# Two per-position convolutions in which the operands of the small products change places: x positions held in the array, the weights moved past them, eight products next to each other

## The chip, the core and the metric

The kernel runs on one core of a Trainium2 chip. The core has a matrix engine (TensorE, PE), a vector engine (DVE), a scalar engine (ACT), GpSimd (POOL), a queue engine that issues DMAs (SyncE, SP), an on-chip memory of 128 partitions (SBUF), a small accumulator memory of eight banks that TensorE writes (PSUM), and DRAM. The metric is the time of one execution on the device, in microseconds. A matrix product takes a stationary operand (loaded first) and a moving operand (streamed past it). A product written in fp32 is run as two loads and two matmul records.

## The reference

Two layers, each `x + conv(gn(x))`. The convolution has its own weights for each batch and position, made by a small network:

```python
S2, B, CI, CO, L, K, A, H = (32, 32, 64, 64, 256, 3, 16, 128)
h = relu(_ln(z @ W1 + b1, g1, be1))
w = (h @ W2 + b2).reshape(B, L, CI, CO, K)
hb = relu(_ln(z @ Wb1 + bb1, gb1, beb1))
bias = (hb @ Wb2 + bb2).transpose(0, 2, 1)
xp = pad(x, ((0, 0), (0, 0), (0, 0), (1, 1)))
x_uf = stack([xp[..., i:i + L] for i in range(K)], axis=-1)
out = einsum('sbilk,bliok->sbol', x_uf, w) + bias[None]
```

`x` has the shape (32 samples s, 32 batches b, 64 channels, 256 positions l), fp32, 67 MB. `gn` takes 32 groups of 8 positions; mean and variance of a group are over all batches, channels and the 8 positions, for each sample.

## The kernel before, in words

Partitions hold (two batches, channel). The work goes over 16 pairs of batches, within a pair over 4 chunks of 64 positions, and within a chunk over 3 taps.

For each tap, `make_weights` makes the weights w[i, o, l] of 64 positions: for each of the 64 outputs o and each batch of the pair, one product with the slice of W2 for that output as the stationary operand (128 hidden x 64 channels in) and the 64 hidden vectors as the moving one (L215). Eight outputs fill a PSUM bank; DVE takes each bank out, adds b2 and writes it to `w` with the output innermost (L222). Three banks (`ps_g`) rotate.

Then `convolve` runs the tap's small products (L236): for each position and each batch, w at that position (64 x 64) is the stationary operand and x at the shifted position (64 channels x 32 samples) the moving one. The taps add up in four banks (`ps_c`). The two batches use the upper and the lower half of the partitions. The next tap's weights are made ahead of a tap's products.

After the third tap, `finish` adds the four banks to x plus bias in place on DVE (L283). In the first layer it also takes the result into running means and squared deviations (`stats`, L118 to L128: DVE, ACT and POOL in turn). `join_stats` makes the group mean and inverse deviation from them with a matrix of 1/128. Before the first layer the same `stats` runs over the whole of x.

POOL normalizes a chunk of x (`normalized`, L204 and L205) and adds the bias (L315). `prepare` makes the hidden vectors and the bias for the next pair, one step after each tap. SP loads a pair's x in one DMA of 4 MB, and stores the result in one. The order on each engine is the planner's, with the order of the program as priority.

Of the kernel before, what the change touches and what calls it, by code (L numbers as in the profile page):

```python
# [12 lines left out]
statistics while they are on chip.  # L13
"""
# [9 lines left out]
FP = mybir.dt.float32  # L24
# [4 lines left out]
DRAM = bass.MemoryType.DRAM  # L29

# [3 lines left out]
LC = 64  # L34
# [5 lines left out]
def conv_layers(ctx: ExitStack, tc: tile.TileContext, x: bass.AP, layers: list, out: bass.AP):  # L40
# [3 lines left out]
    NP = B // 2  # L44
    NCH = L // LC
    GC = LC // E
    NB = LC // 16
    OG = 512 // LC
    assert 2 * C == P and 16 * S == 512 and NB == 4
# [3 lines left out]
    xp = ctx.enter_context(tc.tile_pool(name="x", bufs=2))  # L53
    xnp = ctx.enter_context(tc.tile_pool(name="xn", bufs=2))
# [5 lines left out]
    ps_c = ctx.enter_context(tc.tile_pool(name="ps_c", bufs=NB, space=PSUM))  # L60
    ps_p = ctx.enter_context(tc.tile_pool(name="ps_p", bufs=1, space=PSUM))

    # Centers a column over the 128 partitions; averages it.
    center = const.tile([P, P], FP, name="center")
    make_identity(nc, center)
    nc.vector.tensor_scalar(center, center, 1.0 / P, None, ALU.subtract)
    average = const.tile([P, P], FP, name="average")
    nc.vector.memset(average, 1.0 / P)
    eps = const.tile([P, 1], FP, name="eps")
    nc.vector.memset(eps, EPS)  # L70

    run_mean = const.tile([P, S, G], FP, name="run_mean")
    run_m2 = const.tile([P, S, G], FP, name="run_m2")
    gmean = const.tile([P, S, G], FP, name="gmean")
    rstd = const.tile([P, S, G], FP, name="rstd")

    def rows(t, j):
        return t[:, 2 * j : 2 * j + 2].rearrange("s b c l -> (b c) s l")

    x1 = [dram.tile([P, S, L], FP, name=f"x1_{j}") for j in range(NP)]  # L80

# [24 lines left out]
    def stats(j, y, g0, ng):  # L106
        """Takes y [P, S, ng * E], of pair j, into the running statistics of groups g0 and on."""
        d = prep1.tile([P, S // 2, GC * E], FP, tag="sd", name="sd")
        for h in range(2):
            ss = slice(h * S // 2, (h + 1) * S // 2)  # L110
            ye = y[:, ss].rearrange("p s (g e) -> p s g e", e=E)
            de = d[:, :, : ng * E].rearrange("p s (g e) -> p s g e", e=E)
            mean = run_mean[:, ss, g0 : g0 + ng]
            m2 = run_m2[:, ss, g0 : g0 + ng]
            shape = [P, S // 2, ng]
            m = mean if j == 0 else prep2.tile(shape, FP, tag="sm", name="sm")
            q = m2 if j == 0 else prep2.tile(shape, FP, tag="sq", name="sq")
            nc.vector.tensor_reduce(m, ye, AX.X, ALU.add)  # L118
            nc.scalar.mul(m, m, 1.0 / E)  # L119
            nc.gpsimd.tensor_tensor(de, ye, m[:, :, :, None].to_broadcast(shape + [E]), ALU.subtract)  # L120
            nc.scalar.activation(de, de, AF.Square)  # L121
            nc.vector.tensor_reduce(q, de, AX.X, ALU.add)  # L122
            if j:
                nc.vector.tensor_tensor(m, m, mean, ALU.subtract)  # L124
                nc.vector.scalar_tensor_tensor(mean, m, 1.0 / (j + 1), mean, ALU.mult, ALU.add)  # L125
                nc.vector.tensor_tensor(m2, m2, q, ALU.add)  # L126
                nc.scalar.activation(m, m, AF.Square, scale=(E * j / (j + 1)) ** 0.5)  # L127
                nc.vector.tensor_tensor(m2, m2, m, ALU.add)  # L128

    def join_stats():  # L130
        """gmean and rstd, the same on every partition."""
        n = E * NP
        flat = {k: v.rearrange("p s g -> p (s g)") for k, v in (("m", run_mean), ("q", run_m2), ("g", gmean), ("r", rstd))}
        for h in range(S * G // 512):
            c = slice(h * 512, (h + 1) * 512)
            pm = ps_p.tile([P, 512], FP, tag="pp", name="pm")
            nc.tensor.matmul(pm, average, flat["m"][:, c], start=True, stop=True)  # L137
            nc.scalar.copy(flat["g"][:, c], pm)
            d = prep1.tile([P, 512], FP, tag="hsq", name="sdev")
            nc.vector.tensor_tensor(d, flat["m"][:, c], flat["g"][:, c], ALU.subtract)  # L140
            nc.scalar.activation(d, d, AF.Square)
            v = prep1.tile([P, 512], FP, tag="hc", name="svar")
            nc.vector.scalar_tensor_tensor(v, flat["q"][:, c], 1.0 / n, d, ALU.mult, ALU.add)
            pv = ps_p.tile([P, 512], FP, tag="pp", name="pv")
            nc.tensor.matmul(pv, average, v, start=True, stop=True)
            nc.scalar.activation(flat["r"][:, c], pv, AF.Sqrt, bias=eps)
            nc.vector.reciprocal(flat["r"][:, c], flat["r"][:, c])  # L147

    def prepare(par, t, j, res):
        """The hidden vectors and the bias of pair j into res, in steps for the tensor engine."""  # L150
        N = 2 * L
        A = par["z"].shape[0]
        zt = prep2.tile([A, N], FP, tag="zt", name="zt")
        nc.sync.dma_start(out=zt, in_=par["z"][:, j * N : (j + 1) * N])
        for net in ("w", "b"):
            w, b, g, be = t[net]
            p1 = ps_p.tile([P, N], FP, tag="pp", name="p1")
            nc.tensor.matmul(p1, w, zt, start=True, stop=True)
            h = prep1.tile([P, N], FP, tag="hh", name="hh")
            nc.scalar.activation(h, p1, AF.Identity, bias=b)  # L160
            yield
            p2 = ps_p.tile([P, N], FP, tag="pp", name="p2")
            nc.tensor.matmul(p2, center, h, start=True, stop=True)  # L163
            hc = prep1.tile([P, N], FP, tag="hc", name="hc")
# [191 lines left out]
```

## Time and profile before

| | |
|---|---|
| median of 3 runs | 8146.04 us (8134.46 to 8150.21) |
| span of the profiled execution | 8109.2 us |
| TensorE busy, matmul records | 6764.3 us, 197136 |
| DVE busy | 4705.8 us |
| POOL busy | 2349.0 us |
| ACT busy | 661.3 us |
| moved by DMA | 375.27 MB, mean 46 GB/s |
| mean granted TensorE clock | 0.852 |

The span runs from the first to the last instruction of one profiled execution; no other time of that execution is given, and the median of the runs is 37 us above its span. In the rows, "PE" is a matmul and "PEld" the load of its stationary operand; L215 is line 215; "pc<-xn,w" is what is written and what is read; "128x512 f32" are partitions and elements; the mean of one instruction is in ns. "PEclk" is the granted TensorE clock in tenths of full speed, in 40 equal slices of the span.

### The profile page before, as it was taken

The page shows a single profiled execution, that of the slowest core. Times are in us where ns is not written, and L with a number is a line of the kernel's source. Part 1 is how long each engine was busy: PE and PEld are TensorE (multiplying, and loading weights), DVE is VectorE, ACT ScalarE, POOL GpSimd, SP SyncE. Part 2 cuts the span into 40 slices and gives each one's busy share as a digit, 9 for nine tenths or more (in the row PEclk, how much of TensorE's full clock was granted, in tenths as well). Part 3 has the DMA queues.
Part 4 walks back from the last instruction along what each step waited for, and adds up shares of the span by engine and source line. Part 5 has one row for each costly group of instructions (what it writes and reads, how often), then busy time and mean ns, then how long its engine had stood idle before and what let it go on. Part 6 is the DMA issues. An engine that isn't in the chain of part 4 may idle for free.

```text
span 8109.2 us, 402907 instructions
## 1 busy us (share of the span) xinstructions
PE 6764.3 (83%) x197136; PEld 6501.6 (80%) x197136; DVE 4705.8 (58%) x5199; ACT 661.3 (8%) x1118; POOL 2349.0 (29%) x1094
## 2 busy tenths in 40 slices
PE   2006888888888888888888889999999999999998
PEld 1005888788887888888878789999999999999998
DVE  7996555555555555555555545555555555555554
ACT  3331000000000000000000000000000000000000
POOL 3443322222322222222222313222222222322222
PEclk8556888788888888788878879999999999999999
DMA  4331110111001110111011110111111111111111
GB/s 151 110 104 43 45 45 3 44 45 44 16 32 45 45 41 6 44 45 44 3 44 45 45 75 4 45 45 45 46 46 46 46 46 46 49 47 40 45 45 45
DMA packets 208263, 375.27 MB, mean 46 GB/s; under 512 B 4352, under 2 KB 201280, under 8 KB 201792
## 3 DMA queue, kind: packets, MB, share of 16 engines
q1 hardware_dynamic: 206656, 349.49, 12.9%
q8 instruction: 1540, 25.23, 1.3%
q14 instruction: 67, 0.55, 0.0%
HBM read 215.26 MB, written 134.22 MB: 43 GB/s over the span
## 4 chain that ended last, share of the span: by engine, by line
PE 75%; DVE 11%; POOL 11%; issue 2%; ACT 1%; DMA 0%; SPq 0%; DVEq 0%; POOLq 0%; ACTq 0%
PE pc L236 40%; PE pg L215 33%; POOL xn L205 4%; POOL xn L204 3%; DVE run_m L128 2%; DVE sq L122 2%; POOL sd L120 2%; DVE sm L118 2%; POOL xt L315 2%; DVE sm L124 1%; DVE w L222 1%; DVE run_mean L125 1%; PE p L170 1%; DVE run_m L126 1%; PE p L163 1%
## 5 line engine op out<-in xcount | busy, mean ns | idle before, releaser
L222 DVE TENSOR_TENSOR w<-pg,b 128x512 f32<-128x512 f32 x3072 | 2987.6, 1075 | 2304.3 <-PE pg L215 2295.4
L215 PE MATMUL pg<-hTw,w 128*64 128x64 f32 x98304 | 3226.9, 231 | 658.0 <-DVE w L222 630.4
L215 PEld LDWEIGHTS pg<-hTw,w 128*64 128x64 f32 x98304 | 3142.4, 146 | 721.4 <-DVE w L222 663.3
L236 PEld LDWEIGHTS pc<-xn,w 64*64 64x64 f32 x98304 | 3291.3, 149 | 231.1 <-issue 185.7
L236 PE MATMUL pc<-xn,w 64*64 64x32 f32 x98304 | 3347.4, 231 | 68.2 <-issue 65.3
L204 POOL TENSOR_TENSOR xn<-xt,gmean 128x2048 f32<-128x2048 f32 (+1 forms) x320 | 534.4, 1712 | 2718.3 <-PE pc L236 2682.2
L205 POOL TENSOR_TENSOR xn<-xn,rstd 128x2048 f32<-128x2048 f32 (+1 forms) x320 | 730.0, 2311 | 2.9 <-DVE rstd L147 2.9
L120 POOL TENSOR_TENSOR sd<-xt,sm 128x1024 f32<-128x1024 f32 x240 | 486.5, 2027 | 506.5 <-DVE sq L122 391.3
L283 DVE TENSOR_TENSOR xt<-pc,xt 128x512 f32<-128x512 f32 x512 | 329.9, 686 | 478.2 <-PE pc L236 478.2
L315 POOL TENSOR_TENSOR xt<-xt,bias 128x2048 f32<-128x2048 f32 x128 | 578.6, 4530 | 0.0
L137 PE MATMUL pm<-run_mean,average 128*128 128x512 f32 x8 | 6.4, 890 | 463.2 <-DVE run_mean L125 462.3
L199 POOL MEMSET xn<- 128x32 f32 x32 | 4.0, 125 | 1304.2 <-PE pc L236 1304.2
L124 DVE TENSOR_TENSOR sm<-sm,run_mean 128x128 f32<-128x128 f32 x240 | 129.3, 539 | 434.6 <-POOL sd L120 434.6
L137 PEld LDWEIGHTS pm<-run_mean,average 128*128 128x128 f32 x8 | 1.6, 249 | 465.1 <-issue 462.5
L121 ACT ACTIVATE sd<-sd 128x1024 f32<-128x1024 f32 x256 | 270.5, 1057 | 867.9 <-POOL sd L120 867.9
L195 POOL MEMSET xn<- 128x32 f32 x32 | 4.0, 125 | 1091.6 <-PE pc L236 1091.6
L122 DVE TENSOR_REDUCE sq<-sd 128x128 f32<-128x1024 f32 x240 | 289.6, 1207 | 1.9 <-ACT sd L121 1.9
L118 DVE TENSOR_REDUCE sm<-xt 128x128 f32<-128x1024 f32 x240 | 285.0, 1208 | 3.4
L128 DVE TENSOR_TENSOR run_m<-run_m,sm 128x128 f32<-128x128 f32 x240 | 233.8, 974 | 20.6 <-ACT sm L127 17.5
L173 DVE RECIPROCAL hsd<-hsd 128x512 f32<-128x512 f32 x64 | 214.5, 3352 | 50.7 <-ACT hsd L172 50.7
L119 ACT ACTIVATE sm<-sm 128x128 f32<-128x128 f32 x240 | 74.3, 310 | 1579.1 <-DVE sm L118 1579.1
L126 DVE TENSOR_TENSOR run_m<-run_m,sq 128x128 f32<-128x128 f32 x240 | 172.9, 720 | 0.1
(44 smaller groups left out, 904.9 us busy)
## 6 DMA issues: line engine op xcount, KB each, us to landing
xt<-in_x_dram SPq DMA_DIRECT2D x32, 4096.0 KB, 19.0
x<-xt SPq DMA_DIRECT2D x16, 4096.0 KB, 13.1
xt<-x SPq DMA_DIRECT2D x16, 4096.0 KB, 13.5
out_dram<-xt SPq DMA_DIRECT2D x16, 4096.0 KB, 17.5
w<-in_L_conv_W_dram SPq DMA_DIRECT2D x6, 2048.0 KB, 12.2
zt<-in_L_conv_z_dram SPq DMA_DIRECT2D x32, 32.0 KB, 1.8
b<-in_L_conv_b_dram SPq DMA_DIRECT2D x4, 48.0 KB, 2.2
Wb<-in_L_conv_Wb_dram SPq DMA_DIRECT2D x2, 32.0 KB, 1.8
```

The lines of the kernel that those rows point to most:

```text
L118: nc.vector.tensor_reduce(m, ye, AX.X, ALU.add)
L120: nc.gpsimd.tensor_tensor(de, ye, m[:, :, :, None].to_broadcast(shape + [E]), ALU.subtract)
L121: nc.scalar.activation(de, de, AF.Square)
L122: nc.vector.tensor_reduce(q, de, AX.X, ALU.add)
L128: nc.vector.tensor_tensor(m2, m2, m, ALU.add)
L204: nc.gpsimd.tensor_tensor(o, i, gmean[:, :, g : g + ng, None].to_broadcast(shape), ALU.subtract)
L205: nc.gpsimd.tensor_tensor(o, o, rstd[:, :, g : g + ng, None].to_broadcast(shape), ALU.mult)
L215: nc.tensor.matmul(pg[h * C : h * C + C, o, :], w2[k][:, o0 + o, :], hT[:, h * L + c * LC : h * L + (c + 1) * LC], start=True, stop=True,)
L222: nc.vector.tensor_tensor(w[:, :, o0 : o0 + OG].rearrange("p l o -> p o l"), pg, t["b2"][:, k, o0 : o0 + OG, None].to_broadcast([P, OG, LC ...
L236: nc.tensor.matmul(banks[l // 16][r, l % 16, :], w[r, l, :], xn[r, l + k, :], start=(k == 0 and l % 16 == 0), stop=(k == K - 1), skip_grou ...
L283: nc.vector.tensor_tensor(yq, banks[j, c][q].rearrange("p l s -> p s l"), yq, ALU.add)
L315: nc.gpsimd.tensor_tensor(y, y, b, ALU.add)
```

## The change

The work goes over 32 single batches, with two chunks for each. Partitions hold (half of the positions, channel) for x and the weights. The positions of a half are cut into four quarters of 32, which makes eight eighths in all; a chunk is 16 positions of each of the eight.

`convolve` now takes x at one position (64 channels x 32 samples) as the stationary operand and moves the weights of up to three outputs past it, 3 x 64 columns: position m adds to the results at m-1, m and m+1, with the matching tap of each. Eight products follow each other, one for each eighth: two halves of the partitions (rows of the array) by four quarters (groups of 32 columns). Results have (quarter, sample) on the partitions, one bank for each half and group of 8 positions.

All three taps' weights of a chunk are in one tile, `wall`, with four slots, of which a chunk uses three; the order of the taps alternates, so that the first tap made for a chunk goes to the slot that the chunk before does not use. `make_weights` has the same products as before, with the 64 moving columns taken from four quarters; the eviction now writes eight outputs next to each other.

Since the results lie by (quarter, sample) and x by channel, `addend` adds the bias to x on POOL, writes it to DRAM (`xb`) and reads it back as `y` in eight DMAs with runs of 32 positions. `finish` adds the banks to `y`, in the first layer takes bn_stats of each part, and `store` writes `y` in eight DMAs. `load` fetches a batch in two DMAs with one more position at the inner edge. `x` has one buffer, `xn` and `y` two.

The statistics of x come from bn_stats over tiles in which partitions hold (four batches, sample). The order on TensorE and DVE is the program's; the other queues keep the planner's.

```diff
-    xp = ctx.enter_context(tc.tile_pool(name="x", bufs=2))
+    xp = ctx.enter_context(tc.tile_pool(name="x", bufs=1))
     xnp = ctx.enter_context(tc.tile_pool(name="xn", bufs=2))
-    wp = ctx.enter_context(tc.tile_pool(name="w", bufs=2))
+    wp = ctx.enter_context(tc.tile_pool(name="w", bufs=1))
+    yp = ctx.enter_context(tc.tile_pool(name="y", bufs=2))
+    dram2 = ctx.enter_context(tc.tile_pool(name="dram2", bufs=2, space=DRAM))
+    ps_c = ctx.enter_context(tc.tile_pool(name="ps_c", bufs=2 * NB, space=PSUM))
...
+    def first_stats(stage):
+        parts = stage.tile([P, G, 2 * B // NT, 6], FP, name="parts")
+        CH = C // 2
+        for q in range(B // NT):
+            for h in range(2):
+                t = stage.tile([P, CH, L], FP, tag="xs", name="xs", bufs=3)
+                for k in range(NT):
+                    nc.sync.dma_start(
+                        out=t[k * S : (k + 1) * S], in_=x[:, q * NT + k, h * CH : (h + 1) * CH, :]
+                    )
+                for g in range(G):
+                    nc.vector.bn_stats(parts[:, g, 2 * q + h, :], t[:, :, g * E : (g + 1) * E])
...
+    def addend(xt, bias):
+        i = xt[:, :, 1 : H + 1]
+        nc.gpsimd.tensor_tensor(i, i, bias[:, None, :].to_broadcast([P, S, H]), ALU.add)
+        xb = dram2.tile([S, C, L], FP, tag="xb", name="xb")
+        for r in range(2):
+            nc.sync.dma_start(
+                out=xb[:, :, r * H : (r + 1) * H].rearrange("s c l -> c s l"), in_=i[r * C : (r + 1) * C]
+            )
+        y = yp.tile([P, 2, C, LT], FP, tag="y", name="y")
+        for r in range(2):
+            for t in range(NT):
+                l0 = r * H + t * LT
+                nc.sync.dma_start(out=y[t * S : (t + 1) * S, r], in_=xb[:, :, l0 : l0 + LT])
+        return y
...
-            nc.vector.tensor_tensor(
-                w[:, :, o0 : o0 + OG].rearrange("p l o -> p o l"),
-                pg,
-                t["b2"][:, k, o0 : o0 + OG, None].to_broadcast([P, OG, LC]),
+            nc.vector.tensor_tensor(
+                wall[:, kk + c, :, o0 : o0 + OG],
+                pg.rearrange("p o l -> p l o"),
+                t["b2"][:, k, None, o0 : o0 + OG].to_broadcast([P, NP, OG]),
                 ALU.add,
             )
+            tick()
...
+    def convolve(xn, c):
+        pc = [[ps_c.tile([P, E, C], FP, tag="pc", name="pc") for _ in range(NB)] for _ in range(2)]
+        for m in range(-1, LC + 1):
+            lo, hi = max(m - 1, 0), min(m + 2, LC)
+            for q in range(lo // E, (hi - 1) // E + 1):
+                n0, n1 = max(lo, q * E), min(hi, (q + 1) * E)
+                for t in range(NT):
+                    for r in range(2):
+                        nc.tensor.matmul(
+                            pc[r][q][t * S : (t + 1) * S, n0 - q * E : n1 - q * E, :],
+                            xn[r * C : (r + 1) * C, t * LT + c * LC + m + 1, :],
+                            moved(r, t, c, m, n0, n1),
+                            start=(m == q * E - 1),
+                            stop=(m == (q + 1) * E),
+                            skip_group_check=True,
+                        )
+        return pc
...
+            for b in range(B):
+                for c in range(NCH):
+                    order = (0, 1, 2) if c == 0 else (2, 1, 0)
+                    for step, kk in enumerate(order):
+                        make_weights(t, w2, res[b]["w"], c, kk, tick)
+                        if step == 0:
+                            if before:
+                                products(*before)
+                            before = (b, c)
+                            if c == 0 and b + 1 < B:
+                                res[b + 1] = {}
+                                xns[b + 1] = normalized(xt)
+                                steps = prepare(par, t, b + 1, res[b + 1])
+                    if c == 0 and b + 1 < B:
+                        for _ in steps:
+                            pass
+                        ys[b + 1] = addend(xt, res[b + 1]["bias"])
+                        if b + 2 < B:
+                            xt = load(src, b + 2)
```

Here S = 32, C = 64, H = 128, LT = 32, LC = 16, NT = 4, E = 8, NB = 2, NP = 64, OG = 8 and NCH = 2.

More of the change, by code (lines that the diff above doesn't have):

```diff
@@ L29 @@
 DRAM = bass.MemoryType.DRAM
+ENG = mybir.EngineType
 P = 128
@@ L33 @@
 G = 32
-LC = 64
+NT = 4
+LC = 16
 EPS = 1e-5
@@ L104, in small_weights @@
         return t
[L106 to L147, printed above, removed]
@@ L250, in given, with big_weights @@
[L250 to L265 removed]
+    def big_weights(par):
         w2 = []
@@ new lines, in finish, with products, tick @@
+    def finish(pc, y, b, c, stats):
+        for q in range(NB):
+            for r in range(2):
+                g = c * NB + q
+                part = y[:, r, :, g * E : (g + 1) * E]
+                nc.vector.tensor_tensor(part, pc[r][q].rearrange("p n o -> p o n"), part, ALU.add)
+                if stats:
+                    nc.vector.bn_stats(between[:, r, g, b, :], part)
+    with tc.manual_schedule(engines={ENG.PE, ENG.DVE}):
+        for n, par in enumerate(layers):
+            t, last = small[n], n == len(layers) - 1
+            src, to = (x1 if n else x), (out if last else x1)
+            w2 = big_weights(par) if n else w2_first
+            if n:
+                next_stats()
+            res = {0: {}}
+            xt = load(src, 0)
+            for _ in prepare(par, t, 0, res[0]):
+                pass
+            xns = {0: normalized(xt)}
+            ys = {0: addend(xt, res[0]["bias"])}
+            xt = load(src, 1)
+            steps = iter(())
+            before = None
+            def products(b, c):
+                pc = convolve(xns[b], c)
+                finish(pc, ys[b], b, c, not last)
+                if c == NCH - 1:
+                    store(ys[b], to, b)
+            def tick():
+                next(steps, None)
+            for b in range(B):
[12 more added lines that the diff above has]
+                    if c == 0 and b + 1 < B:
+                        for _ in steps:
+                            pass
+                        ys[b + 1] = addend(xt, res[b + 1]["bias"])
+                        if b + 2 < B:
+                            xt = load(src, b + 2)
+            products(*before)
```

354 lines of the change are left out of this document (194 added, 160 removed).

## The prediction

> **What bounds the kernel now.** I read the page first (busy shares, granted clock, chain of work), then a table of four stretches, then the timeline of TensorE where its clock is full.
>
> ```profile
> span 8109.2 us, 402907 instructions
> PE 6764.3 (83%) x197136; PEld 6501.6 (80%) x197136; DVE 4705.8 (58%) x5199; ACT 661.3 (8%) x1118; POOL 2349.0 (29%) x1094
> PEclk8556888788888888788878879999999999999999
> PE pc L236 40%; PE pg L215 33%; POOL xn L205 4%; POOL xn L204 3%; DVE run_m L128 2%; DVE sq L122 2%; POOL sd L120 2%; DVE sm L118 2%; POOL xt L315 2%; DVE sm L124 1%; DVE w L222 1%; DVE run_mean L125 1%; PE p L170 1%; DVE run_m L126 1%; PE p L163 1%
> ```
>
> The chain is TensorE for 75%: the small products (L236) 40%, the making of weights (L215) 33%. The stretches, cut at the first product, the layer change and the end (columns: length, then busy time of each engine, clock, DMA share, GB/s):
>
> ```profile
> 0.00:690.00 690.00, 60.47 (x636) 39.23 (x636) 606.05 (x765) 223.87 (x396) 279.13 (x141) 0.59 0.40 119
> 690.00:4730.00 4040.00, 3419.04 (x95440) 3294.01 (x95440) 2254.83 (x2505) 310.64 (x528) 1131.37 (x533) 0.82 0.10 34
> 4730.00:4820.00 90.00, 84.09 (x2214) 82.75 (x2212) 43.32 (x53) 3.66 (x7) 4.06 (x3) 0.78 0.20 73
> 4820.00:8109.00 3289.00, 3200.70 (x98858) 3085.63 (x98854) 1801.64 (x1878) 123.11 (x188) 934.46 (x417) 0.94 0.14 45
> ```
>
> Three parts: 690 us of statistics with TensorE almost idle and DVE busy 606; the first layer, 4040 us, in which DVE also carries the statistics; the second, 3289 us, TensorE busy 97% of it. In the first layer TensorE waits for DVE's evictions:
>
> ```profile
> PE pg L215 <- DVE w L222: 584.3, 119, 13.0
> ```
>
> The pace of TensorE at full clock, one tap's weights and one tap's products (256 matmul records each, two per written fp32 product), and one stretch after a gap in issue:
>
> ```profile
> 6998.74 7.68 PE L215 MATMUL pg<-hTw,w 128*64 128x64 f32 x256
> 3000.34 7.66 PE L236 MATMUL pc<-xn,w 64*64 64x32 f32 x256
> 5294.08 12.73 PE L236 MATMUL pc<-xn,w 64*64 64x32 f32 x242 [2.94 <-issue]
> ```
>
> Both kinds go at 30 ns a record. The third row is the half clock that a gap of 3 us sets off: some 5.5 us lost on a tap.
>
> **The products.** Written products fall from 49152 to 160 for each batch and 64-position chunk: 16 positions in each of 8 tiles, at 18 places with two more where a place crosses a bank, times 8. With 128 such chunks that is 20480, 40960 records. Each now moves up to 192 columns (three outputs of 64) against 32, but each tile is 64 rows by 32 columns of the array, eight of them next to each other. Do they overlap? Two rows bear on it: one full-width product of 512 columns, and the two half-width products of 256 columns of L182.
>
> ```profile
> 7143.52 1.12 PE L170 MATMUL p<-hsq,average 128*128 128x512 f32 x2
> 7006.25 0.60 PE L182 MATMUL p<-hTb,Wb 128*64 128x256 f32 x4
> ```
>
> One after the other the two of L182 would take as long as the 512 columns, 1.12 us; they took 0.60. So products on different columns run side by side, passes included. 1.12 / 512 is 2.2 ns a column. A chunk has 3072 columns per tile (16 positions x 3 x 64), so 6.7 us if all eight run together. The other bound is issue: 320 records at 30 ns are 9.6 us. I take 8 us, between them.
>
> [...]
>
> **The weights.** As many records as before (49152 products, 64 columns moved): a batch has six taps-by-chunks of 7.68, 46.1 us. `wall` has one buffer, but step 0 of a chunk writes the slot that the products before it do not read, and the other steps' evictions stand behind those products anyway. The hidden vectors cost a batch six products of 256 columns (half of 1.12) and two small ones, about 4 us. TensorE per batch: 46.1 + 2 x 8 + 4 = 66 us.
>
> **DVE and POOL.**
>
> ```profile
> L222 DVE TENSOR_TENSOR w<-pg,b 128x512 f32<-128x512 f32 x3072 | 2987.6, 1075 | 2304.3 <-PE pg L215 2295.4
> L283 DVE TENSOR_TENSOR xt<-pc,xt 128x512 f32<-128x512 f32 x512 | 329.9, 686 | 478.2 <-PE pc L236 478.2
> L173 DVE RECIPROCAL hsd<-hsd 128x512 f32<-128x512 f32 x64 | 214.5, 3352 | 50.7 <-ACT hsd L172 50.7
> L205 POOL TENSOR_TENSOR xn<-xn,rstd 128x2048 f32<-128x2048 f32 x128 | 684.5, 5347 | 2.9 <-DVE rstd L147 2.9
> L315 POOL TENSOR_TENSOR xt<-xt,bias 128x2048 f32<-128x2048 f32 x128 | 578.6, 4530 | 0.0
> L204 POOL TENSOR_TENSOR xn<-xt,gmean 128x2048 f32<-128x2048 f32 x128 | 489.2, 3822 | 2718.3 <-PE pc L236 2682.2 <-ACT gmean L138 36.1
> 660.62 1.22 DVE L118 TENSOR_REDUCE sm<-xt 128x128 f32<-128x1024 f32 x1
> 661.76 0.28 DVE L124 TENSOR_TENSOR sm<-sm,run_mean 128x128 f32<-128x128 f32 x1
> ```
>
> The first six rows are groups (count, then busy, mean ns of one), the last two single instructions.
>
> The eviction of the weights (same count, 48 a batch) now writes runs of 8 outputs instead of single elements 256 bytes apart. L283 also reads PSUM with a stride, writes runs of 16 and takes 686 against 1075 ns: I take 0.69, bounds 0.69 and 1.08. With 8 additions of 0.69, reciprocals half as wide (2 x 1.7) and, in the first layer, 8 bn_stats of 512 elements (not in the trace; 0.69, as for the other 512-element work, at most the 1.2 of a 1024-element reduction), DVE needs 33 + 5.5 + 4 + 5.5 = 48 us a batch, 67 at the upper bound. Below TensorE's 66 or level with it, so the 584 us of waiting go. The running statistics of before (L118 to L128) go with them.
>
> POOL works on 4096 elements a batch, so twice its rows: 2 x (3.82 + 5.35 + 4.53) = 27.4 us. That is little, but it now stands in a loop with the DMAs.
>
> **The new transfers.** This is what speaks against the change. Results lie by (eighth, sample) on the partitions and x by channel, so x plus bias goes out to `xb` in DRAM and comes back as `y`. A batch has 4096 pieces of 516 bytes (load), 4096 of 512 (to `xb`), 16384 of 128 (back into `y`) and 16384 of 128 (store). The `x` pool has one buffer, so these follow each other: `addend` on POOL, `xb` written, then, both behind that write on the one queue and `y` first, the reads of `y` and the load of the batch after next, then its `normalized`, then its `addend`. The store can use the time in which POOL works.
>
> What does a 128-byte piece cost? The nearest rows: a window of 0.4 us in which one load of 128 pieces of 256 bytes and some of 4 bytes ran, and one store of 4096 pieces of 1 KB.
>
> ```profile
> DMA packets 194, 0.03 MB, mean 83 GB/s; under 512 B 194, under 2 KB 194, under 8 KB 194
> q1 hardware_dynamic: 194, 0.03, 43.0%
> DMA packets 4112, 4.19 MB, mean 293 GB/s; under 512 B 16, under 2 KB 4112, under 8 KB 4112
> q1 hardware_dynamic: 4112, 4.19, 96.8%
> zt<-in_L_conv_z_dram SPq DMA_DIRECT2D x32, 32.0 KB, 1.8
> xt<-in_x_dram SPq DMA_DIRECT2D x32, 4096.0 KB, 19.0
> ```
>
> 194 packets in 0.4 us are 2.1 ns each, with the engines 43% busy: 0.9 ns if they could be filled, which is the lower bound. The store took 14.3 us, 3.5 ns a piece, engines full; a 128-byte piece should not cost more: upper bound. I take 1.6 (nearest the first row, whose window has idle edges) and 2.2 for 512 bytes. Then the loop is: `xb` 4096 x 2.2 = 9 and about 2 to land; `y` 26 + 2; load 9 + 2; POOL 27.4, which just covers the store's 26. Sum 78 us. That is over TensorE's 66, so the transfers set the pace, with TensorE late by some 12 us a batch; gaps that long bring the half clock, and 5.5 us for one or two of them still fit under 78. For queueing I take 80 us a batch.
>
> **Statistics and ends.** Before the first layer 512 bn_stats of 256 elements replace the chain of 606 us; at about 0.42 (between 0.28 for 128 elements and 0.69 for 512) that is 215 us. x is 16 times 4 MB: 229 us at 14.3, 304 at the 19.0 that the loads took. I take 270, and 50 for merging and spreading: 320, range 270 to 400.
> Each layer starts with a load, a normalization and three steps of weights uncovered, and ends with a store: 80 us each. Sum: 320 + 64 x 80 + 2 x 80 = 5600 us of span. The median of the runs, 8146, lies 37 over the span of 8109; with it 5637, say 5640.
>
> **The rivals.**
> (a) The transfers hide. If the pieces cost under about 1.3 ns each, the loop is 24576 x 1.3 + 27 + 6 = 65 and TensorE's 66 binds: 64 x 66 + 480 + 37 = 4740 us. For it: engines 43% busy in the 256-byte window. Against: neither window goes under 2 ns.
> (b) Slower, by one mechanism: the small pieces. Break-even is (8109 - 480) / 64 = 119 us a batch. If the store no longer fits under POOL, the loop is 32768 pieces and 24 us more, 119 at 2.9 ns a piece. At 3.5, the whole price of the 1 KB pieces, it is 139 us and 64 x 139 + 517 = 9410 us. For it: in large DMAs no piece here went faster than 3.5 ns. Against: there the engines were full with bytes.
> [...]
> (c) The eight products go only in pairs, as the pairs of before do. Then a chunk takes up to 4 x 6.7 = 27 us, some 24 without start-up, TensorE 46 + 48 + 4 = 98 a batch: 64 x 98 + 517 = 6790 us. For it: only two are shown. Against: the pair of L182 cost hardly more than one.
> (d) Evictions stay at 1.08: DVE 67 us a batch, still under 80; alone this changes (a) by a few us a batch.
>
> **How the numbers follow.** Transfer loop near 80 us: 0.42. (a) 0.28. (c) 0.12. (b) 0.18. The likeliest gives 5640. Its own range, 1.3 to 2.4 ns a piece (71 to 104 us), is 5060 to 7170. For 8 in 10 the range takes in (a) with the lower bound of the statistics, and (c), and leaves (b) out: 4500 to 7700. The runs before spread over 0.2%, so that is what counts as no change. All cases but (b) are faster: 0.82; within 0.2% 0.01; slower 0.17.
>
> **What would show it.** Right: the loads of x and the reads of `y` among the longest waits, POOL's L204-like work waiting for a DMA, a batch every 80 us, DMA share over 0.6, the products' 320 records in about 8 us, evictions near 0.69, first product near 380 us. Wrong: TensorE busy without gaps and 66 us a batch (a); a batch over 119 us (b); a chunk's products at 20 us or more (c); evictions at 1.08; or statistics beyond 400 us because a load into 32 partitions is slower than one into 128.

## Result, and the profile after

The changed kernel takes 6796.55 us (median of 4 runs, 6774.26 to 6809.7) against 8147.27 in the same series: a ratio of 0.8336, 95% interval 0.8313 to 0.836. The forecast was 5640 with a range of 4500 to 7700. The direction and the range held; the likeliest value was 17% too low, and not for the reason that the prediction had in mind.

The page of the changed kernel (span, TensorE's row, shares of the queues, the chain by engine and by line):

```profile
span 6806.9 us, 289596 instructions
PE 4626.3 (68%) x140322; PEld 4231.2 (62%) x140322; DVE 3263.5 (48%) x4649; ACT 332.3 (5%) x725; POOL 1735.7 (25%) x462
GB/s 193 226 84 110 76 102 87 77 92 90 93 74 102 88 74 95 90 90 76 102 86 87 109 83 82 95 84 87 88 93 71 96 90 76 91 91 93 71 101 54
q1 hardware_dynamic: 2650688, 619.05, 59.2%
q8 instruction: 1096, 17.96, 1.3%
PE 65%; issue 15%; DVE 8%; DMA 7%; SPq 5%; ACT 1%; POOL 0%; DVEq 0%; POOLq 0%; ACTq 0%
PE pg L340 47%; PE pc L367 13%; SPq L330 5%; DMA xs<-in_x_dram 4%; DVE hc L256 3%; DVE hsd L255 3%; DMA zt<-in_L_conv_z_dram 2%; PE p L242 2%; PE p L250 1%; PE p L236 1%; DVE wall L343 1%; DMA w<-in_L_conv_W_dram 1%; PE p L265 1%; ACT hTb L259 1%; DVE y L382 0%
```

TensorE is still first on the chain, but now "issue" is second with 15%: time in which an engine waited for nothing that the profile shows. Of the batches' transfers only the issue of the stores (L330, 5%) and the z behind it (2%) stand there; xb, y and the loads of x do not. The groups (busy, mean ns of one, then idle time before them and what ended most of it):

```profile
L340 PE MATMUL pg<-hTw,w 128*64 128x64 f32 x98304 | 3440.0, 236 | 651.7 <-issue 527.0
L343 DVE TENSOR_TENSOR wall<-pg,b 128x512 f32<-128x512 f32 x3072 | 2104.0, 690 | 2282.8 <-PE pg L340 2277.5
L367 PE MATMUL pc<-wall,xn 64*32 64x192 f32 (+2 forms) x40960 | 898.0, 314 | 452.7 <-issue 451.5
L305 POOL TENSOR_TENSOR xn<-xt,gmean 128x4096 f32<-128x4096 f32 x64 | 474.1, 7408 | 2434.8 <-PE pc L367 2270.7
L236 PE MATMUL p<-zt,W 16*128 16x256 f32 x128 | 55.6, 520 | 399.4 <-DMA zt<-in_L_conv_z_dram 398.1
L169 DVE BATCH_NORM_STATS2 parts<-xs 128x6 f32<-128x256 f32 x512 | 168.6, 408 | 197.5 <-DMA xs<-in_x_dram 150.2
L256 DVE TENSOR_TENSOR hc<-hc,hsd 128x256 f32<-128x256 f32 x128 | 251.4, 1964 | 4.4
L175 PE MATMUL am_ps<-am,quarter 128*128 128x32 f32 x2 | 0.6, 411 | 371.8 <-DVE am L126 371.8
L265 PE MATMUL p<-hTb,Wb 128*64 128x128 f32 x256 | 40.8, 414 | 242.5 <-ACT hTb L259 242.5
```

And where the products begin and end (first and last start):

```profile
L367 PE MATMUL pc<-wall,xn x40960: 212/322/527, 462.8 to 6786.9; 64*32 64x192 f32 x119, 64*32 64x64 f32 x42, 64*32 64x128 f32 x39
```

From the first product to the last are 6324 us, 98.8 a batch with the layer change spread over them (later "us a batch" is this quotient). The rows fill it: weights 3440.0 / 64 = 53.8, products 14.0, waits for issue (527.0 + 451.5) / 64 = 15.3, waits for z 6.2, for hTb 3.8, for evictions (651.7 - 527.0) / 64 = 1.9, and some 5 for the products of the hidden vectors. POOL, on the other hand, waits for TensorE (2270.7 us), hardly for loads (150 us in all): the loop of transfers is not what paces.

What "issue" is shows in TensorE's timeline (start, length, line, records, idle time before):

```profile
5007.99 2.21 PE L367 MATMUL pc<-wall,xn 64*32 64x64 f32 x109
5010.37 2.55 PE L367 MATMUL pc<-wall,xn 64*32 64x192 f32 x128 [0.18 <-issue]
5014.11 1.82 PE L367 MATMUL pc<-wall,xn 64*32 64x192 f32 x83 [1.20 <-issue]
5066.12 4.30 PE L367 MATMUL pc<-wall,xn 64*32 64x64 f32 x128 [5.77 <-issue]
5085.77 3.95 PE L340 MATMUL pg<-hTw,w 128*64 128x64 f32 x128 [0.34 <-issue]
5092.25 3.95 PE L340 MATMUL pg<-hTw,w 128*64 128x64 f32 x128 [2.54 <-issue]
5100.93 6.37 PE L340 MATMUL pg<-hTw,w 128*64 128x64 f32 x164 [4.73 <-issue]
```

The stretches between gaps have 128 records or a multiple of it, products and weights counted together (behind the 83 products stand 45 weights). With the loads 128 records are 256 instructions, and the queue "instruction" moved 1096 packets: 2 x 140322 / 256 = 1096. By this count TensorE's instructions come in by DMA in blocks of 256, 16 KB each (17.96 MB / 1096). That the gaps are waits for these blocks shows in the trace's packets: of the 572 issue gaps behind 400 us, nine in ten end between 1.27 and 1.66 us after a packet of that queue has landed, though the packets start 4.7 us apart (median). Products at 20 ns a record (2.55 us for 128) use a block up faster than the next one arrives (one every 3.74 us in the run with split products below). The weights at 30 ns (3.95 us for 128) wait 527.0 us for issue here, and at most 396.3 - 355.0 = 41 in the run without big transfers. The block at 5066.12 took 4.30 us behind its gap, at a granted clock of 0.57.

### The profile page after: what moved, and what is told of

Read it like the earlier page. It is cut to its first block, busy times and chain, and to the rows that moved or that the text cites. A ratio compares the mean times of both kernels' runs of the same rounds, so it can differ in the third digit from the quotient of the medians.

```text
span 6806.9 us, 289596 instructions
## 1 busy us (share of the span) xinstructions
PE 4626.3 (68%) x140322; PEld 4231.2 (62%) x140322; DVE 3263.5 (48%) x4649; ACT 332.3 (5%) x725; POOL 1735.7 (25%) x462
## 3 DMA queue, kind: packets, MB, share of 16 engines
q8 instruction: 1096, 17.96, 1.3%
## 4 chain that ended last, share of the span: by engine, by line
PE 65%; issue 15%; DVE 8%; DMA 7%; SPq 5%; ACT 1%; POOL 0%; DVEq 0%; POOLq 0%; ACTq 0%
PE pg L340 47%; PE pc L367 13%; SPq L330 5%; DMA xs<-in_x_dram 4%; DVE hc L256 3%; DVE hsd L255 3%; DMA zt<-in_L_conv_z_dram 2%; PE p L242 2%; PE p L250 1%; PE p L236 1%; DVE wall L343 1%; DMA w<-in_L_conv_W_dram 1%; PE p L265 1%; ACT hTb L259 1%; DVE y L382 0%
## 5 line engine op out<-in xcount | busy, mean ns | idle before, releaser
L340 PE MATMUL pg<-hTw,w 128*64 128x64 f32 x98304 | 3440.0, 236 | 651.7 <-issue 527.0
L343 DVE TENSOR_TENSOR wall<-pg,b 128x512 f32<-128x512 f32 x3072 | 2104.0, 690 | 2282.8 <-PE pg L340 2277.5
L367 PE MATMUL pc<-wall,xn 64*32 64x192 f32 (+2 forms) x40960 | 898.0, 314 | 452.7 <-issue 451.5
L367 PEld LDWEIGHTS pc<-wall,xn 64*32 64x32 f32 x40960 | 772.8, 113 | 561.8 <-issue 526.1
L305 POOL TENSOR_TENSOR xn<-xt,gmean 128x4096 f32<-128x4096 f32 x64 | 474.1, 7408 | 2434.8 <-PE pc L367 2270.7
L382 DVE TENSOR_TENSOR y<-pc,y 128x512 f32<-128x512 f32 x512 | 339.7, 684 | 993.8 <-PE pc L367 990.2
L313 POOL TENSOR_TENSOR xt<-xt,bias 128x4096 f32<-128x4096 f32 x64 | 524.5, 8195 | 1096.5 <-ACT bias L267 1096.5
L305 POOL TENSOR_TENSOR xn<-xn,rstd 128x4096 f32<-128x4096 f32 x64 | 663.7, 10371 | 5.0
L256 DVE TENSOR_TENSOR hc<-hc,hsd 128x256 f32<-128x256 f32 x128 | 251.4, 1964 | 4.4
L175 PE MATMUL am_ps<-am,quarter 128*128 128x32 f32 x2 | 0.6, 411 | 371.8 <-DVE am L126 371.8
L175 PEld LDWEIGHTS am_ps<-am,quarter 128*128 128x128 f32 x2 | 0.5, 313 | 371.8 <-DVE am L126 371.8
L255 DVE RECIPROCAL hsd<-hsd 128x256 f32<-128x256 f32 x128 | 223.0, 1743 | 14.2 <-ACT hsd L252 14.2
```

Source lines behind the costliest of these rows:

```text
L255: nc.vector.reciprocal(sd, sd)
L256: nc.vector.tensor_tensor(hc, hc, sd, ALU.mult)
L305: nc.gpsimd.tensor_tensor(o, i, st[:, :, 1 : GH + 1, None].to_broadcast(shape), op)
L313: nc.gpsimd.tensor_tensor(i, i, bias[:, None, :].to_broadcast([P, S, H]), ALU.add)
L340: nc.tensor.matmul(pg[r * C : r * C + C, o, :], w2[k][:, o0 + o, :], h[:, r, :, c, :], start=True, stop=True)
L343: nc.vector.tensor_tensor(wall[:, kk + c, :, o0 : o0 + OG], pg.rearrange("p o l -> p l o"), t["b2"][:, k, None, o0 : o0 + OG].to_broadcast ...
```

## The experiments

Theory A at first: the 128-byte pieces delay the blocks and z. B: every transfer that fills the DMA engines delays the blocks. C: the loop of transfers and POOL paces, as predicted. Unless something else is said, each run is the changed kernel with one edit; ratios are to the kernel before, the changed kernel's being 0.8336.

**Long pieces.** `y` is read and stored as 16 KB pieces.

```diff
-                nc.sync.dma_start(out=y[t * S : (t + 1) * S, r], in_=xb[:, :, l0 : l0 + LT])
+            nc.sync.dma_start(out=yf[t * S : (t + 1) * S], in_=xb[:, t * CQ : (t + 1) * CQ, :].rearrange("s c l -> s (c l)"))
```

> The reads of y and the stores move the same bytes in pieces of 16 KB instead of 128 bytes (four DMAs each instead of eight; so each value of x is added to a result at another place, and results land at other places). Theory A, TensorE sets the pace and the 128-byte pieces delay its instruction fetches and z: its waits for issue fall from 978 us to under 400, the wait for z from 398 to under 100, time 5.6 to 6.0 ms. Theory B, any transfer that fills the DMA engines delays the fetches, whatever its pieces: the waits during the load and the write of xb (570 us) stay, those during the 128-byte pieces (290) go, and z comes early: 6.1 to 6.4 ms. Theory C, the loop of transfers sets the pace as forecast: it shrinks by 14 us of y to some 64 us and TensorE's 66 binds, 4.7 ms.

Measured 6738.22 us, 0.8269 (0.8242 to 0.8295). The groups of this run:

```profile
L344 PE MATMUL pg<-hTw,w 128*64 128x64 f32 x98304 | 3489.1, 238 | 933.0 <-issue 721.1
L371 PE MATMUL pc<-wall,xn 64*32 64x192 f32 (+2 forms) x40960 | 892.4, 313 | 482.5 <-issue 481.2
L256 DVE TENSOR_TENSOR hc<-hc,hsd 128x256 f32<-128x256 f32 x128 | 359.8, 2811 | 4.4
```

The waits for z are gone, and what they left was taken by issue (979 to 1202 us) and by DVE. The size of the pieces is not the cause: A falls. B's range is missed too: the 290 us of issue waits that it laid to the small pieces did not go.

**No round trip.** `xb`, the reads of `y` and the stores are left out; both layers read x.

```diff
-        return y
+        return y_all
...
-            src, to = (x1 if n else x), (out if last else x1)
+            src, to = x, out
```

> xb, the reads of y and all stores but the last are left out (the results pile up in one tile of y, both layers read the input x, and only the last batch of the output is written). Theories A and B: what is left is TensorE with the loads and z alone: 46 us of weights, two chunks of products at 8 to 10, 5.5 for the hidden vectors, some 5 us of gaps during the load: 74 to 80 us a batch, 5.2 to 5.6 ms. If the products' own pace outruns the fetch of instructions even without transfers, gaps of at least 100 us stay in the products. Theory C: the loop is load 16 and POOL 27 only, so TensorE's 66: 4.7 ms.

Measured 6105.33 us, 0.7497 (0.7475 to 0.7518), 87.7 us a batch:

```profile
L332 PE MATMUL pg<-hTw,w 128*64 128x64 f32 x98304 | 3300.1, 233 | 420.3 <-DVE wall L335 340.6
L359 PE MATMUL pc<-wall,xn 64*32 64x192 f32 (+2 forms) x40960 | 899.1, 315 | 506.9 <-issue 505.9
```

With three of the four transfers gone a batch still takes 87.7, far from C's 66 and above the 74 to 80 that A and B gave. The weights hardly wait for issue any more, the products as much as ever: of their 506 us, 375 lie in the 883 us in which the one remaining transfer, the load of x, is on the engines (the gaps laid over the trace's packets, microsecond by microsecond). In its place waits for DVE have come up.

**z on ScalarE's queue.**

```diff
-        nc.sync.dma_start(out=zt, in_=par["z"][:, b * L : (b + 1) * L])
+        nc.scalar.dma_start(out=zt, in_=par["z"][:, b * L : (b + 1) * L])
```

> The load of z is issued from ACT, so that it does not stand behind the stores on SP's queue. Theories A and B: TensorE's wait for z (398 us, 20 times) goes under 100, and with it some half clock: 6.25 to 6.5 ms. Theory C, the loop of transfers paces: z is no part of the loop, 6.7 to 6.85 ms.

Measured 6428.98 us, 0.7892 (0.7871 to 0.7913). Here the predicted picture does appear; the waits of POOL and of SP's queue:

```profile
POOL xn L305 <- DMA xt<-x: 1557.7, 31, 55.9
POOL xn L305 <- DMA xt<-in_x_dram: 1536.5, 30, 64.3
SPq L323 <- DMA zt<-in_L_conv_z_dram: 1368.9, 56, 35.7
```

POOL now waits for loads, 3094 us, which it did not before. The loop has grown: the reads of `y` stop half-way for the z on the other queue, 24 us each time (39.16 us for the eight reads in one batch, 18.55 in the changed kernel). The trace shows what ties the two together: the program gives its DMAs semaphores in turn, and in that batch the fifth read has the one that z's DMA has. It waits for z to land, and ScalarE issues z only at 5046.23, after the first four reads, which ended at 5024.57. A batch takes 92.8 us, the 70 of the loop (worked out below) and most of these 24. So the loop paces in this run, though its time lies in the range of A and B; in the changed kernel POOL's waits for loads, which would show it, are missing. The kernel still gains 368 us, in keeping with the z wait being off TensorE and `hc` hardly meeting POOL any more (602 ns on the mean).

**One quarter after another.** The loop over the quarters stands outside, so that at most two of the eight products are side by side.

```diff
+        for t in range(NT):
         for m in range(-1, LC + 1):
...
-                for t in range(NT):
```

> The same products, but all of one quarter before the next, so that only the two halves of the partitions can run side by side. If eight ran side by side before: a chunk's products go from 7 us busy to 22 to 27 us, the gaps in issue inside them go, and the time rises by 128 x 12 to 16 us, to 8.3 to 8.9 ms. If they ran in pairs anyway: 6.8 ms, unchanged.

Measured 7903.72 us, 0.9699 (0.9673 to 0.9725):

```profile
L367 PE MATMUL pc<-wall,xn 64*32 64x192 f32 (+2 forms) x40960 | 2586.9, 291 | 6.8 <-issue 6.1
```

A chunk takes 2586.9 / 128 = 20.2 us, under the 22 to 27 expected, instead of 7.0 plus 3.5 of gaps. If two at a time take 20.2, then 7.0 takes some six at a time on the mean: more than four side by side is real, and worth 1107 us. At 63 ns a record the gaps before products fall from 452 to 6 us, although all transfers are still there: products slower than the blocks no longer feel them. The weights, still at their old pace, wait 355 us for issue.

**The old order of the evictions.**

```diff
-                wall[:, kk + c, :, o0 : o0 + OG],
-                pg.rearrange("p o l -> p l o"),
+                wall[:, kk + c, :, o0 : o0 + OG].rearrange("p l o -> p o l"),
+                pg,
```

> The eviction is iterated as in the kernel before (output by output, positions inside, written 256 bytes apart); all else as in the changed kernel. If the order of writing is what made it faster, one eviction takes about 1.07 us again instead of 0.69, and DVE has some 69 us of work in a batch of 99. Theory (TensorE and the arrival of its instructions set the pace): most of the 3072 x 0.38 = 1170 us stays beside TensorE; 6800 to 7050 us, the wait of the weights for evictions rises from 119 to 200 to 350 us. Rival (evictions stand on TensorE's path): all of it shows, about 7950 us. If the eviction stays at 0.69 the order was not the cause, and the time is 6797.

Measured 6826.74 us, 0.8384 (0.8343 to 0.8425), an interval that overlaps the changed kernel's.

```profile
L343 DVE TENSOR_TENSOR wall<-pg,b 128x512 f32<-128x512 f32 x3072 | 3001.9, 1063 | 1460.6 <-PE pg L340 1453.7
```

The order of writing makes the eviction faster (690 against 1063 ns), and 898 us of DVE buy some 30 us, which the intervals do not tell from nothing: DVE's idle time in front of it shrinks from 2283 to 1461 us instead.

**Statistics over two queues.**

```diff
-                    nc.sync.dma_start(
+                    (nc.sync if k < 2 else nc.scalar).dma_start(
```

> Two of the four loads of each statistics tile are issued from ScalarE's queue instead of SyncE's; nothing else moves. If one queue's loads into 32 partitions each run alone (40 us for 8 MB, 187 GB/s) because that queue works them off one after the other, two at a time are faster: first product at 220 to 270 us instead of about 400, 6620 to 6680 us in all. Rival: the loads already overlap and the reading itself is the limit: first product unmoved, 6780 to 6810 us.

Measured 6771.59 us, 0.8316 (0.8268 to 0.8364). The wait of L175 for the statistics is 369.9 us (371.8 before): the rival is right in that the one queue is not the limit; the time lies just under its range.

**z ahead.** z is loaded a batch earlier on the same queue.

```diff
                         if b + 2 < B:
+                            zt = load_z(par, b + 2)
                             xt = load(src, b + 2)
```

> The z of a batch is loaded a batch earlier, on the same queue, behind the reads of y and ahead of the load of x; the issue queues stay as they are otherwise. Theory (TensorE with the arrival of its instructions paces, z was one further wait of about 400 us, and the stall of the reads of y in the run with z on ScalarE's queue came from that queue change): the z wait goes, the issue waits stay near 1000 us, POOL does not wait for loads, 6250 to 6420 us. Rival (once z is gone the loop of transfers and POOL takes over, as it did in the run with z on ScalarE's queue): POOL waits for loads again, 6420 to 6500 us. Second rival (z hides other waits that return): 6600 us or more.

Measured 6509.75 us, 0.7995 (0.7953 to 0.8037): 287 us faster, less than the 398 of the z waits and just above the range of either of the first two expectations. POOL does not wait for loads, so it is not the loop.

```profile
L342 PE MATMUL pg<-hTw,w 128*64 128x64 f32 x98304 | 3431.4, 235 | 712.0 <-issue 497.5
L258 DVE TENSOR_TENSOR hc<-hc,hsd 128x256 f32<-128x256 f32 x128 | 350.2, 2736 | 4.4
```

The rest came back at the evictions: TensorE's waits before the weights, other than issue, rise from 125 to 214 us, and `hc` from 1964 to 2736 ns, because it falls into POOL's work more often: 61 of its 128 instructions are long instead of 41, and each of these ends within 0.3 us of an instruction of POOL.

**No big transfers.** As the run without the round trip, and without the loads of x inside the layers.

```diff
-                        if b + 2 < B:
-                            xt = load(src, b + 2)
```

> As the run without the round trip, but also without the loads of x inside the layers: x of batch 0 is loaded once per layer and normalized again for each batch; POOL, VectorE and TensorE do the same work. Only z still comes in. Theory (transfers delay the fetch of TensorE's instructions): of the 506 us that the products waited for issue in the run without the round trip, 375 lay in the loads; they fall to what the other chunks showed, about 2 us a chunk, 260 us: 5800 to 5900 us. Rival (the gaps are the products' own, a fixed price of running 128 records in 2.55 us): 450 us or more of issue waits remain, 6050 to 6110 us.

Measured 5624.57 us, 0.6905 (0.6871 to 0.6938), 80.3 us a batch; below the range that B gave.

```profile
L332 PE MATMUL pg<-hTw,w 128*64 128x64 f32 x98304 | 3241.3, 231 | 396.3 <-DVE wall L335 355.0
L359 PE MATMUL pc<-wall,xn 64*32 64x192 f32 (+2 forms) x40960 | 809.7, 294 | 219.0 <-issue 217.3
```

The products' gaps fall from 506 to 217 us, as B asked for; that their records and the weights' also got shorter (899 to 810, 3300 to 3241, with the granted clock at 0.924 against 0.892) was left out of the expectation. 1.7 us a chunk are the products' own.

**Split products.** As the run without big transfers, with 384 products of 64 columns instead of 160 of up to 192; the same columns.

```diff
-                for t in range(NT):
+                for j in range(n0, n1):
+                    for t in range(NT):
...
-                            moved(r, t, c, m, n0, n1),
+                                moved(r, t, c, m, j, j + 1),
```

> As the run without big transfers (5625 us), but each product moves the 64 columns of one output position instead of up to 192 of three: the same columns in 384 products a chunk instead of 160, 768 records instead of 320. No transfer stands beside them. Theory (TensorE's instructions arrive in blocks of 256, not faster than one block in about 3.7 us, 29 ns a record): a chunk's products go from 8.0 us with gaps to about 22 us with a gap behind nearly every block; 7250 to 7500 us. Rival (the array's columns set the time, the gaps belong to something else): 5600 to 5750 us.

Measured 7316.13 us, 0.9001 (0.8982 to 0.902): 1691 us slower, for the same columns and with no big transfer beside it; 1644 us of it stand in the products' row. Its page and timeline:

```profile
PE 5150.6 (70%) x197666; PEld 4744.0 (65%) x197666; DVE 3335.2 (46%) x4649; ACT 335.7 (5%) x725; POOL 1729.1 (24%) x339
q8 instruction: 1544, 25.30, 1.4%
L360 PE MATMUL pc<-wall,xn 64*32 64x64 f32 x98304 | 1437.6, 278 | 1234.9 <-issue 1234.2
```

```profile
3089.95 2.04 PE L360 MATMUL pc<-wall,xn 64*32 64x64 f32 x128 [1.71 <-issue]
3093.69 2.04 PE L360 MATMUL pc<-wall,xn 64*32 64x64 f32 x128 [1.71 <-issue]
3097.44 1.73 PE L360 MATMUL pc<-wall,xn 64*32 64x64 f32 x101 [1.71 <-issue]
```

Blocks start every 3.74 us, TensorE works 2.04 of it and stands for 1.71, and 2 x 197666 / 256 = 1544 is the packet count again. So with only z beside it TensorE gets 128 records in 3.74 us, 29 ns a record; a chunk went from (809.7 + 219.0) / 128 = 8.0 us to 20.9.

**The operand in PSUM.** The square root and its reciprocal are written in place into PSUM.

```diff
-            nc.scalar.activation(sd, p3, AF.Sqrt, bias=eps)
+            nc.scalar.activation(p3, p3, AF.Sqrt, bias=eps)
...
-            nc.vector.tensor_tensor(hc, hc, sd, ALU.mult)
+            nc.vector.tensor_tensor(hc, hc, p3, ALU.mult)
```

In the changed kernel, one multiplication beside POOL (both from the timeline):

```profile
5030.71 4.16 DVE L256 TENSOR_TENSOR hc<-hc,hsd 128x256 f32<-128x256 f32 x1
5024.12 10.47 POOL L305 TENSOR_TENSOR xn<-xn,rstd 128x4096 f32<-128x4096 f32 x1
```

It ends at 5034.87, POOL's at 5034.59: it waits for the rest of POOL's instruction. The next one, with POOL idle, takes 0.42 us.

> As the changed kernel, but the square root and its reciprocal are written in place into PSUM, so that the multiplication of L256 reads one operand from SBUF and one from PSUM. Theory (with two SBUF operands it shares a way into SBUF with POOL, and takes 4 us instead of 0.42 while POOL works): the group mean falls from 1964 to 400 to 550 ns, 180 to 200 us of DVE go, and of that the part on the path (4% of the span, some 240 us with what stands behind it): 6600 to 6720 us. Rival (the long ones are waits of another kind, or the fetch of TensorE's instructions fills the time anyway): mean falls but the time stays at 6770 to 6800; or the mean stays.

Measured 6612.65 us, 0.8137 (0.8121 to 0.8153).

```profile
L255 DVE TENSOR_TENSOR hc<-hc,p 128x256 f32<-128x256 f32 x128 | 53.9, 421 | 4.4
L339 PE MATMUL pg<-hTw,w 128*64 128x64 f32 x98304 | 3381.0, 234 | 519.8 <-issue 511.1
```

421 ns each time, TensorE's waits before the weights other than issue fall from 125 to 9 us, and the kernel is 184 us faster. In the changed kernel 41 of the 128 multiplications are long, and each of these ends 0.25 to 0.29 us after an instruction of POOL; with one operand in PSUM none is long (420 to 423 ns). That the two share a way into SBUF, as the expectation has it, was the author's supposition and is not shown.

**All three.** z ahead, the operand in PSUM, and the second net first, with its last product among the weights.

```diff
-        for net in ("w", "b"):
+        for net in ("b", "w"):
...
+            if net == "w":
+                break
...
+            res["bias"] = bias
+            yield
```

> Three changes on top of the changed kernel: z loaded a batch earlier (as in the run z ahead, 6510), the PSUM operand, and the second net computed first with its last product (p4) among the weights, so that TensorE does not stand still for the last activation. Theory (TensorE and the arrival of its instructions pace): of the 6510, about 240 us of waits for hTb, 200 to 260 us of waits behind DVE go, the issue waits of some 950 us stay: 5950 to 6150 us. Rival (the loop of transfers and POOL paces once these are gone, 94 us a batch as in the run with z on ScalarE's queue): 6400 us, POOL waiting for loads.

Measured 6063.85 us, 0.7459 (0.7438 to 0.7481), 87.2 us a batch: the fastest version that does the whole work, 733 us ahead of the changed kernel, and inside the range of the first expectation. Two groups, and POOL's longest wait:

```profile
L343 PE MATMUL pg<-hTw,w 128*64 128x64 f32 x98304 | 3274.7, 229 | 622.0 <-issue 592.6
L370 PE MATMUL pc<-wall,xn 64*32 64x192 f32 (+2 forms) x40960 | 936.3, 322 | 443.7 <-issue 442.3
```

```profile
POOL xn L308 <- PE pc L370: 2616.9, 57, 54.1
```

The issue waits stay, 1035 us, 17% of the span: the largest of TensorE's waits that are left.

**All three, no big transfers.**

```diff
-        return y
+        return y_all
...
-                            xt = load(src, b + 2)
```

> The version with all three changes, without the round trip of the sums through DRAM and without the loads of x inside the layers (as the run without big transfers, which had none of the three changes: 5625 us). What is left is TensorE, VectorE, ScalarE and POOL with only z coming in. Theory (of the 1035 us that the version with all three waits for issue, the transfers cause all but the products' own 1.7 us a chunk): issue waits about 220 us, half clock rarer, 5000 to 5200 us, some 72 us a batch: what the prediction took for TensorE (66) and a few us of gaps. Rival (the transfers only move the waits about, and other work on DVE or POOL binds once they are gone): 5400 us or more, with other waits in their place.

Measured 4963.64 us, 0.6101 (0.6083 to 0.6119), 70.3 us a batch, just below the range expected.

```profile
L335 PE MATMUL pg<-hTw,w 128*64 128x64 f32 x98304 | 3053.1, 223 | 95.8 <-DVE wall L338 50.4
L362 PE MATMUL pc<-wall,xn 64*32 64x192 f32 (+2 forms) x40960 | 817.0, 295 | 216.7 <-issue 215.8
```

So the transfers, none of which TensorE waits for by name, cost the version with all three 1100 us: 1035 - 216 - 45 = 774 or more of issue waits (45 is all that the weights' row leaves to causes other than evictions), and 3274.7 - 3053.1 + 936.3 - 817.0 = 341 of longer records, in keeping with the granted clock (0.934 against 0.987).

## Why the prediction was right or wrong

**TensorE's own work: right, but not in this kernel.** Forecast 46.1 + 16 + 4 = 66 us a batch. Undisturbed (last run) the weights take 47.7, the chunks 2 x 8.1 with gaps; with the hidden vectors and remaining waits 70.3. In the changed kernel it is 98.8. The step of the prediction that failed is "TensorE per batch: ... 66 us" as a number that transfers leave alone. The prediction charged every transfer to the loop of `xt`, none to TensorE. Yet it quoted the row with a gap of 2.94 us "issue", and used it only for the half clock behind it (granted clock 0.52 over the row's 12.73 us, 1.00 over the 34 us ahead; in that kernel's trace behind 690 us, the 3 us after each of TensorE's 89 waits of 3 us or more have 0.50 on the mean); it did not ask what the gap was, or that there would be more of them with 59% DMA share in place of 10 to 14%. Issue waits and longer records against the last run: 15.3 - 4 = 11 and (3440.0 - 3053.1 + 898.0 - 817.0) / 64 = 7.3 us a batch. That 6797 lies in the stated range is owed to the range's width; no case in it had this mechanism.

**"The transfers set the pace": wrong as meant.** The loop was priced at 78 us and measures 70 in the batch of the timeline, with room under TensorE's 98.8 (SP's queue: start, time to issue; below it the page's row for the loads, with the time to landing):

```profile
5056.55 3.55 SPq L316 DMA_DIRECT2D xb<-xt  x2
5064.48 18.55 SPq L323 DMA_DIRECT2D y<-xb  x8
5083.07 2.90 SPq L291 DMA_DIRECT2D xt<-x  x1
5086.02 2.53 SPq L292 DMA_DIRECT2D xt<-x  x1
5016.69 21.76 SPq L330 DMA_DIRECT2D out_dram<-y  x8
```

```profile
xt<-x SPq DMA_DIRECT2D x64, 1032.0 KB, 14.4
```

`xb` 7.9, `y` 18.6, load 17.3, POOL 26.0 (forecast 27.4). A 128-byte piece costs 1.13 ns on the way in and 1.33 on the way out, where 1.6 was taken: below the 1.3 that rival (a) asked for in the one direction, just above it in the other. (At 1.3 ns the prediction has the loop twice, at 65 us in (a), where the pieces of 512 bytes cost 1.3 too, and at 71 as the lower end of its own range.) Rival (b) did not come: the small writes are 17% dearer than the small reads (21.76 against 18.55 us for 16384 pieces).

**The z wait and DVE's wait for POOL: not in the forecast.** z stands on SP's queue behind the store, and that waits for the last results and takes 21.76 us to issue: 6.2 us a batch. The prediction counted the store as hidden under POOL and did not go through the queue for what else stands behind it. The multiplication of L256 was in no term; it and the wait for hTb cost about 6 us a batch. These three are what the version with all three was to take out: the z wait falls to 22 us, the multiplication to 0.42 us, the wait for hTb only from 243 to 83 us.

**Products: the size right, its reason only in part.** A chunk is 7.0 us busy in the changed kernel, and 8.0 with its own gaps where no transfer disturbs it, against 8 forecast. The 30 ns a record that was taken there as a bound of issue was none: undisturbed the records take 19.8 ns (809.7 us for 40960), and 1.7 us of gaps bring the chunk to 8.0. The 160 products belong to a chunk of 128 positions, not of 64 as written; the total of 20480 is right. (c) is excluded in the changed kernel, and what it would do is 7904, not 6790, since it left out the same terms. That 6797 came out beside (c)'s 6790 is chance.

**Evictions, reciprocals, bn_stats: right**, 0.690 (0.69), 1.743 (1.7), 0.694 and 0.408 (0.69 and 0.42) us; and (d) too: the old order costs some 30 us, 0.5 a batch.

**The beginning: low.** The wait for the statistics is 372 us where 270 + 50 were taken, in the range of 270 to 400; the first product comes at 462.8 instead of near 380, since 91 us pass behind that wait where 60 were left for it. Reading goes at 193 and 226 GB/s in the first two slices; the 19.0 us a load of before (304 in all) was the row to take, not a mean with the store's 14.3.

## What to carry to other kernels

Count TensorE's instructions: 256 of them came about every 3.7 us here, and big transfers beside them made it slower (1035 us of issue waits in the version with all three, at most 261 without the transfers), so short records pay for a DMA that nothing waits for by name. A gap marked "issue" that returns every 128 records is that. Fewer transfers shortened these gaps (the products' from 506 to 217 us), and more and shorter products lengthened them (217 to 1234 us); shorter waits elsewhere left them as they were (979 and 1035 us). When a wait is removed, look up what is next in line (of z's 398 us 111 came back, most of it at DVE), and remove them together.

## What was not expected of the hardware

- TensorE's records ran at 16 ns (2.04 us for 128) in the split run and at 20 in the changed kernel, once a block was there; the block's arrival, 29 ns a record, was the limit.
- The packet of a block took 1.09 us on the mean in the run without big transfers and 1.33 in the changed kernel; 0.24 us more for each of 1096 blocks are 263 us, while the issue waits grew by 720 or more (from 258 at most to 979). Where the rest is lost, at the DMA engines or in DRAM, was not tried, and so how a transfer delays a block stays open.
- Loads of x for the statistics, 32 rows 2 MiB apart, went at 193 and 226 GB/s in the first two slices from one queue, and from two the wait for them was the same (369.9 against 371.8 us). Whether the pitch sets this rate no run shows.
